# Making the context's keys and values for two layers in one process of lower rank, kept in DRAM

## The chip, the cores and the metric

The kernel runs on one core of a Trainium2 chip. The time is device microseconds of one launch. Engines are named as in the profile: PE (TensorE matmuls), PEld (its weight loads), DVE (VectorE), ACT (ScalarE), POOL (GpSimd), SP (SyncE, which issues the DMAs here; SPq is its queue).

## The reference

Two decoder layers over 128 sequences of 64 tokens, each token 128 numbers wide, float32. Six residual blocks follow one another; each is fed the layer-normalised `x`:

```
x = x + mamba2_and_mlp(norm(x))
x = x + pointer_attention(norm(x), ctx, ids, pointers)   # reads ctx
x = x + ternary_ffn(norm(x))
x = x + causal_attention(norm(x))                        # attention, convolution, attention
x = x + cross_attention(norm(x), ctx, mask)              # reads ctx
x = x + mixture_of_experts(norm(x))                      # 8 experts, top 2
```

The context `ctx_1024` has the shape of `x` and does not depend on it. Pointer attention lets each token look at three neighbouring context rows in two ways ("j" and "i"); its keys and values are `ctx @ Wkj.T`, `ctx @ Wvj.T` and the same with `i`. Cross attention has 16 heads of 8: `k = ctx @ wk`, `v = ctx @ wv`, softmax of the scores with a mask, then `@ wo`.

## The kernel before

The sequences are cut into 16 groups (`NG`) of 8 sequences (`B`), which are 512 tokens (`GT`), four tiles of 128 (`C`). A group passes ten stages in order (`LAYERS`, L199): `prepare`, `project`, `recur`, `mlp` (the mamba block), `pointers`, `ternary`, `first`, `second` (the causal block), `cross`, `experts`. `way(g)` (L1603) is the process of one group: it takes one of seven `x` buffers, loads the group, goes through the stages, and stores the result. One group at a time can be in a stage, and it leaves a stage only when the next one is free.

The order of all instructions is made while the program is built, by `Turns` (L85), a planner. Each process is a Python generator that yields

- a name: it waits for a token, such as a buffer or a stage; `turns.give(name)` gives it back, to the one who has waited longest;
- a pair of an engine and a cost in us: the instructions that follow are placed on that engine at the planned time;
- `None` and a time: it lets that much planned time pass;
- a list: child processes, all of which must end.

Among those who ask for an engine, the planner takes first the process that holds something scarce (a bank "a" or the score banks "s"), and then the one that asked first (L156, L168). The planner's order is each engine's program order on the chip. SP's instructions stand in the order in which the generators reach them.

Tokens that matter here (L196 and L200): `a`, four PSUM banks; `s`, one set of four more banks for scores; `u`, two buffers for normalised rows; `fT`, six for transposed rows; `km`, four (used by `project` to `recur`, by `first` to `second`, and by `cross`); `qm`, three; `ctxT`, two; `pT`, three sets.

What is done with the context before the change:

- In `pointers`, `group(g)` (L781) takes `ctxT` and a `u`, loads the group's context into it (L786), and runs three things side by side: `context()`, `ones()` (one-hot rows of the pointers) and `norming_T` (normalise `x`, transpose it). `context()` transposes the four tiles into `ctxT` (`turning`, L311 to L320, evacuated by ACT), stores `ctxT` to the DRAM tensor `contexts` (L802), and makes `kT` in two blocks (`keys`, L806: one 512-column matmul with `wqk` and an ACT copy each) and `vo` in two blocks (`outputs`, L815: eight small matmuls with `wvo` and an ACT copy each). `kT` and `vo` have one buffer each and no token. `kT` is read by the scores (L851) and `vo` by the last matmuls of the stage (L936); L943 then adds the result to `x`.
- In `cross`, `group(g)` (L1417) loads `ctxT` back (L1427) and runs side by side `queries()` (normalise, transpose, multiply with `wq`) and `of_context()`: `spreading` (one matmul with `wkk`, two ACT activations into `km`, L1073 to L1092) and `values` (four matmuls with `wv` and four small copies, two on DVE and two on ACT, into the tile `v_x`, whose other elements are zero; L1094). Then `attend` (L1248) reads `km` and `v_x`.
- `weights()` (L1616) prepares the weights of the later layers at the start, layer by layer, and gives each stage's token when its weights are ready.

All float32 matmuls go through the helper at L210, transposes through L317. Each float32 matmul has two records in the profile.

Of the kernel before, what the change touches and what calls it, by code (L numbers as in the profile page):

```python
# [24 lines left out]
F32 = mybir.dt.float32  # L25
# [59 lines left out]
class Turns:  # L85
# [14 lines left out]
    def give(self, name):  # L100

        self.running["scarce"] = max(0, self.running["scarce"] - (name in self.scarce))
        if self.wanted[name]:
            _, process = self.wanted[name].pop(0)
            process["time"] = max(process["time"], self.now)
            process["scarce"] += name in self.scarce
            process["engine"] = None
            self.ready.append(process)
        else:
            self.free[name].append(self.now)  # L110

    def process(self, work, time, parent):
        return dict(work=work, time=time, parent=parent, scarce=0, engine=None, n=0)

    def step(self, process):
        self.running = process
        while True:
# [21 lines left out]
            elif isinstance(item, list):  # L139
                process["children"] = len(item)  # L140
                for work in item:
                    self.ready.append(self.process(work, process["time"], process))
                return
            else:
                engine, length = item
                if engine is None:
                    process["time"] += length
                    process["engine"] = None
                    continue

                process["at"] = process["time"]
                if engine is process["engine"]:
                    process["at"] -= self.LAG
                else:
                    process["engine"], process["n"] = engine, self.n
                self.asked.setdefault(engine, []).append((process["scarce"] < 1, process["n"], process, length))  # L156
                return

    def run(self, works):
        self.ready = [self.process(work, 0.0, None) for work in works]  # L160
        while True:
# [3 lines left out]
            for engine, asked in self.asked.items():  # L165
                if asked:
                    at = max(self.until.get(engine, 0.0), min(r[2]["at"] for r in asked))
                    first = min((r for r in asked if r[2]["at"] <= at), key=lambda r: r[:2])  # L168
                    if best is None or at < best[0]:
# [4 lines left out]
            self.asked[engine].remove(request)  # L174
            process, length = request[2:]
            self.until[engine] = at + length
# [6 lines left out]
def tile_decoder(ctx: ExitStack, tc: tile.TileContext, w: dict, const: bass.AP, out: bass.AP):  # L183
# [16 lines left out]
    TOKENS = dict(BUFS, a=4, s=1, pT=3, mx=3)  # L200
    TOKENS.update({name: int(i < 4) for i, name in enumerate(LAYERS)})
    counter = [0]
    pools = {}
# [38 lines left out]
    xs = [None] * NG  # L242
    contexts = dram.tile([NG * P, GT], F32, tag="contexts", name="contexts")

# [479 lines left out]
    def pointers(mp):  # L724
# [56 lines left out]
        def group(g):  # L781

            yield "ctxT"
            yield "u"
            cg = wk([P, C, P], "u", bufs=BUFS["u"])
            nc.sync.dma_start(cg, tokens(cf, g))  # L786
            ctxT = wk([P, GT], "ctxT", bufs=BUFS["ctxT"])
            idg = wk([P, C, S], "idg", I32)
            for b in range(2):
                nc.sync.dma_start(  # L790
                    idg[b * S : (b + 1) * S], ids[b, g * C : (g + 1) * C, :].partition_broadcast(S)
                )
            kT = wk([P, B, 2, S], "kT")
            vo = wk([P, B, P], "vo")
            hot = wk([P, 3, C, S], "hot")
            rid = sm([P, C], "rid")

            def context():
                yield None, 2.5
                yield from turning(ctxT, [cg[:, c, :] for c in range(C)])  # L800
                turns.give("u")
                nc.sync.dma_start(contexts[g * P : (g + 1) * P, :], ctxT)  # L802
                yield [keys(0), keys(1), outputs(0), outputs(1)]
                turns.give("ctxT")

            def keys(i):  # L806
                yield "a"
                pk = bank("a")
                yield T, 0.88
                mm(pk, wqk[:, i, :], ctxT)  # L810
                yield A, ac(512)
                A.copy(kT[:, :, i, :], pk.rearrange("p (b s) -> p b s", s=S))
                turns.give("a")

            def outputs(half):  # L815
                yield "a"
                pvo = bank("a")
                yield T, 0.95
                for j in range(4):
                    b = half * 4 + j  # L820
                    for i in range(2):
                        mm(
                            pvo[i * S : (i + 1) * S, j * P : (j + 1) * P],
                            ctxT[:, b * S : (b + 1) * S],
                            wvo[:, i, :],
                        )
                yield A, ac(512)
                A.copy(vo[:, half * 4 : half * 4 + 4, :], pvo.rearrange("p (b d) -> p b d", b=4))
                turns.give("a")

# [14 lines left out]
            uT = []  # L845
            yield [context(), ones(), norming_T(xs[g], uT)]
            yield "a"
            psc = bank("a")
            yield T, 0.95
            for b in range(B):  # L850
# [4 lines left out]
                )  # L855
            turns.give("fT")

            s3 = sm([P, 3, 2, C], "s3")
# [76 lines left out]
            for b in range(B):  # L935
# [4 lines left out]
                )  # L940
            turns.give("fT")
            yield V, dv(512)
            V.tensor_tensor(xs[g], xs[g], po_.rearrange("p (c d) -> p c d", c=C), ALU.add)  # L943
            turns.give("a")

        stages["pointers"] = group
        return ready

# [458 lines left out]
    def cross(mp):  # L1407
# [6 lines left out]
        def ready():  # L1414
            vs.extend((yield from value_tiles(mp, "x", 1)))

        def group(g):  # L1417

            mask = wk([P, B, S], "mask")
            for i in range(2):  # L1420
# [3 lines left out]
                )  # L1424
            yield "ctxT"
            ctxT = wk([P, GT], "ctxT", bufs=BUFS["ctxT"])
            nc.sync.dma_start(ctxT, contexts[g * P : (g + 1) * P, :])  # L1427
            v = vs[0]
            yield "km"
            km = wk([P, B, 2, S], "km", bufs=BUFS["km"])  # L1430
            yield "qm"
            qm = wk([P, B, 2, S], "qm", bufs=BUFS["qm"])
# [6 lines left out]

            def of_context():  # L1440
                yield None, 2.5
                yield [spreading(km, wkk, ctxT, k["mk"], None), values(v, ctxT, wv)]

            yield [queries(), of_context()]
            turns.give("ctxT")
            yield "fT"
            oT = wk([P, GT], "fT", bufs=BUFS["fT"])
            yield from attend(masked_weights, qm, km, v, mask, oT)
            turns.give("km")
            yield from projecting(g, oT, wo)  # L1450

        stages["cross"] = group
        return ready

# [148 lines left out]
    def way(g):  # L1603
# [10 lines left out]
        turns.give("x")  # L1614

    def weights():  # L1616

# [4 lines left out]
        for ready, names in zip(layers, (LAYERS[4:5], LAYERS[5:6], LAYERS[6:8], LAYERS[8:9], LAYERS[9:10])):  # L1622
            yield from ready()
            for name in names:
                turns.give(name)
        for _ in range(2):
            turns.give("pT")
# [4 lines left out]
    with tc.manual_schedule(engines={e.engine for e in (V, A, G, T)}):  # L1632
        turns.run([way(g) for g in range(NG)] + [weights()])

# [20 lines left out]
```

## Time and profile before

| | us |
|---|---|
| median of 3 runs (2209.86 to 2229.43) | 2220.43 |
| the profiled execution | 2218.08 |
| its span, first to last instruction | 2216.3 |
| PE busy | 1925.3 (87%) |
| DVE busy | 1489.0 (67%) |
| PEld busy | 1363.1 (62%) |
| ACT busy | 1158.7 (52%) |
| POOL busy | 1020.8 (46%) |
| mean granted TensorE clock | 0.931 |
| data moved by DMA | 53.61 MB, mean 24 GB/s |

The profile page is read from the top: busy time of each engine, then 40 equal slices of the span (each digit is a slice's busy share in tenths; PEclk is the clock that was granted to PE), then the DMA queues, then the chain of work that ended last, followed back from the last instruction, then groups of instructions by source line and tiles (busy time, mean ns of one, idle time before them and who ended it), then DMA issues with the time from issue to landing. Durations are of that one execution.

### The profile page before, as it was taken

The numbers are of one execution on the slowest core, as the hardware profiler recorded it, in microseconds if no ns is written. First come the engines' busy times: TensorE is split into PE (matmuls) and PEld (weight loads), VectorE is DVE, ScalarE is ACT, GpSimd is POOL, SyncE is SP. The second block draws the span as 40 slices with busy tenths as digits, with TensorE's granted clock in tenths as the row PEclk, the third lists the DMA queues.
The fourth block names the chain that finished last, engine by engine and source line by source line (L and its number), as shares of the span: only waits on it lengthen the run. The fifth ranks groups of instructions, "written<-read, shape, count | busy, mean of one in ns | idle before, by whom it ended". The sixth has DMA issues, their size and how long they took to land.

```text
span 2216.3 us, 56830 instructions
## 1 busy us (share of the span) xinstructions
PE 1925.3 (87%) x23920; PEld 1363.1 (62%) x23920; DVE 1489.0 (67%) x3991; ACT 1158.7 (52%) x2133; POOL 1020.8 (46%) x1258
## 2 busy tenths in 40 slices
PE   3777788889889989999998898989889999997996
PEld 1455556566656666666666576666556666675664
DVE  4577877675685676786776847777676765745353
ACT  2345456556464566556565464555655555553452
POOL 2566754743444444364545552464544533423121
PEclk9688898999999999999999899999899999998998
DMA  5011010000010010010001000000000000000000
GB/s 164 20 51 36 28 38 2 23 7 18 22 36 12 6 47 21 16 37 15 26 23 38 6 28 21 16 19 26 28 25 24 2 25 11 17 7 6 12 6 5
DMA packets 73451, 53.61 MB, mean 24 GB/s; under 512 B 30087, under 2 KB 59757, under 8 KB 73197
## 3 DMA queue, kind: packets, MB, share of 16 engines
q1 hardware_dynamic: 73196, 49.99, 7.6%
q8 instruction: 188, 3.08, 0.6%
q14 instruction: 67, 0.54, 0.1%
HBM read 41.45 MB, written 8.52 MB: 23 GB/s over the span
## 4 chain that ended last, share of the span: by engine, by line
PE 55%; DVE 26%; POOL 6%; ACT 6%; issue 3%; DMA 3%; SPq 1%; DVEq 0%; POOLq 0%; ACTq 0%
PE psa L210 38%; PE pss L210 12%; PE psa L317 4%; DVE tops L1212 4%; POOL u L325 2%; DVE amx L1167 2%; DVE pT L1155 2%; DVE x L1581 2%; DVE st L307 1%; ACT pT L1245 1%; DVE mv L308 1%; DVE sel L863 1%; DMA x<-in_x 1%; DVE s L870 1%; DVE mx L1030 1%
## 5 line engine op out<-in xcount | busy, mean ns | idle before, releaser
L325 POOL TENSOR_SCALAR u<-x,mv,rstd 128x128 f32<-128x128 f32 x320 | 252.8, 802 | 52.3 <-PE psa L317 26.0
L210 PE MATMUL psa<-fT,moe_w 128*128 128x512 f32 x512 | 257.8, 627 | 11.3 <-ACT km L559 3.1
L210 PEld LDWEIGHTS psa<-moe_w,hid 128*128 128x128 f32 x2048 | 242.5, 193 | 28.6 <-issue 19.1
L210 PE MATMUL psa<-moe_w,hid 128*128 128x128 f32 x2048 | 252.0, 279 | 2.4 <-DVE sel L863 1.7
L1559 ACT ACTIVATE hid<-psa,vcol 128x512 f32<-128x512 f32 x256 | 173.5, 689 | 147.2 <-PE psa L210 144.4
L1581 DVE SCALAR_TENSOR_TENSOR x<-psa,cw,x 128x128 f32<-128x128 f32 x512 | 143.3, 342 | 127.6 <-PE psa L210 127.5
L1169 POOL TENSOR_TENSOR pT<-pT,amx 128x512 f32<-128x512 f32 x128 | 134.6, 1055 | 185.9 <-DVE amx L1167 177.9
L286 POOL TENSOR_SCALAR rsq<-mv 128x4 f32<-128x4 f32 x96 | 24.7, 257 | 368.6 <-DVE mv L308 346.1
L1245 ACT ACTIVATE pT<-pss 128x512 f32<-128x512 f32 x256 | 132.1, 603 | 118.8 <-PE pss L210 118.7
L1212 DVE TENSOR_REDUCE tops<-pss 128x32 f32<-128x2048 f32 x64 | 146.1, 2283 | 41.3 <-PE pss L210 41.3
L1044 POOL TENSOR_SCALAR r<-h 128x512 bf16<-128x512 f32 x64 | 98.0, 1540 | 128.2 <-DVE h L1042 127.0
L210 PEld LDWEIGHTS psa<-fT,moe_w 128*128 128x128 f32 x512 | 91.3, 198 | 100.2 <-issue 59.4
L1289 DVE TENSOR_TENSOR fT<-psa,inv 128x256 f32<-128x256 f32 x96 | 40.2, 420 | 155.2 <-ACT inv L1287 154.2
L210 PEld LDWEIGHTS pss<-km,qm 32*128 32x128 f32 x3072 | 101.4, 198 | 46.7 <-issue 31.5
L210 PE MATMUL psa<-pT,cst 128*32 128x256 f32 x1536 | 119.6, 401 | 10.4 <-ACT pT L1245 2.9
L625 POOL TENSOR_TENSOR qm<-qm,km 128x256 f32<-128x256 f32 x64 | 51.6, 809 | 165.6 <-DVE qm L620 165.5
L317 PE MATMUL psa<-cst,u 128*128 128x128 f32 x448 | 83.9, 304 | 50.1 <-POOL u L325 33.9
L210 PE MATMUL pss<-km,qm 32*128 32x128 f32 x3072 | 120.6, 297 | 5.6 <-DVE pT L1155 3.5
L307 DVE BATCH_NORM_STATS2 st<-x 128x6 f32<-128x128 f32 x384 | 102.7, 267 | 20.6 <-DMA x<-in_x 20.1
L319 ACT COPY fT<-psa 128x512 f32<-128x512 f32 x112 | 65.7, 588 | 85.2 <-PE psa L317 84.8
L317 PEld LDWEIGHTS psa<-cst,u 128*128 128x128 f32 x448 | 56.0, 151 | 78.2 <-POOL u L325 43.3
L1285 ACT ACTIVATE inv<-psa 128x256 f32<-128x256 f32 x96 | 37.0, 385 | 125.9 <-PE psa L210 125.5
(282 smaller groups left out, 4621.3 us busy)
## 6 DMA issues: line engine op xcount, KB each, us to landing
pT<-steps SPq DMA_DIRECT2D x64, 256.0 KB, 4.0
x<-in_x SPq DMA_DIRECT2D x16, 256.0 KB, 2.8
mask<-in_mask_Bx1xSxS_ff SPq DMA_DIRECT2D x32, 128.0 KB, 3.0
u<-in_ctx SPq DMA_DIRECT2D x16, 256.0 KB, 2.7
contexts<-ctxT SPq DMA_DIRECT2D x16, 256.0 KB, 2.0
ctxT<-contexts SPq DMA_DIRECT2D x16, 256.0 KB
out<-x SPq DMA_DIRECT2D x16, 256.0 KB, 2.3
idg<-in_itok_BxS SPq DMA_DIRECT2D x32, 64.0 KB, 2.8
```

Source lines behind the costliest of these rows:

```text
L210: T.matmul(o, lhsT=lhsT, rhs=rhs, start=start, stop=stop)
L307: V.bn_stats(st[:, c, :], X[:, c, :])
L317: T.transpose(pt[:, c * P : (c + 1) * P], part, by)
L319: A.copy(o, pt)
L325: G.tensor_scalar(u[:, c, :], X[:, c, :], mean(c), scale[:, c : c + 1], ALU.subtract, ALU.mult)
L625: G.tensor_tensor(xc[:, :, cols], xc[:, :, cols], zs[:, :, cols], ALU.mult)
L1044: G.tensor_scalar(r2, h[:, c, :], -MAGIC, None, ALU.add)
L1169: G.tensor_tensor(s3, s3, mx.unsqueeze(2).to_broadcast([P, 8, S]), ALU.subtract)
L1212: V.tensor_reduce(mx[:, :, 0:8], banks.rearrange("p r (n s) -> p r n s", s=S), AX.X, ALU.max)
L1245: A.activation(pTs[r].rearrange("p b g q -> p (b g q)"), banks[:, r, :], AF.Exp)
L1559: A.activation(hid[:, b, :], ph, AF.Relu, bias=vec["moe_b1"][:, 2 * e + b : 2 * e + b + 1])
L1581: V.scalar_tensor_tensor(X[:, c, :], po_[:, c * P : (c + 1) * P], cw[:, c, e : e + 1], X[:, c, :], ALU.mult, ALU.add,)
```

## The change

A new process `ahead` runs beside the 16 ways and `weights`. It goes over all groups in order: it loads a group's context, transposes it into `ctxT`, and makes `kT`, `vo`, `km` and the tile `v_x` of that group, each of which it stores in a DRAM tensor of its own (`kept`). `pointers` loads `kT` and `vo` from there and `cross` loads `v_x` and `km`. `contexts` and the context's use of `u` are gone. `kT`, `vo` and `v_x` now have a token each, with one copy; `pointed{g}` and `crossed{g}` say that a group's tensors are stored; "laid" says that the pointer layer's weights are ready. Every process has a rank: `ahead` has 1, the others 0. A lower number goes first among those who wait for a token, and, after the holders of something scarce, among those who ask for an engine.

```diff
@@ Turns
         if self.wanted[name]:
-            _, process = self.wanted[name].pop(0)
+            first = min(self.wanted[name], key=lambda w: (w[1]["rank"], w[0]))
+            self.wanted[name].remove(first)
+            process = first[1]
...
-                self.asked.setdefault(engine, []).append((process["scarce"] < 1, process["n"], process, length))
+                self.asked.setdefault(engine, []).append(
+                    ((process["scarce"] < 1, process["rank"], process["n"]), process, length)
+                )
@@ tile_decoder
+    TOKENS.update(ctxT=1, kT=1, vo=1, v_x=1, laid=0)
+    TOKENS.update({f"{name}{g}": 0 for name in ("pointed", "crossed") for g in range(NG)})
...
-    contexts = dram.tile([NG * P, GT], F32, tag="contexts", name="contexts")
+    kept = {
+        (name, g): dram.tile([P, n], F32, tag=f"{name}{g}", name=f"{name}{g}")
+        for name, n in (("kT", B * 2 * S), ("vo", B * P), ("km", B * 2 * S), ("v_x", B * 4 * 48))
+        for g in range(NG)
+    }
@@ pointers
         def group(g):
-            yield "ctxT"
-            yield "u"
-            cg = wk([P, C, P], "u", bufs=BUFS["u"])
-            nc.sync.dma_start(cg, tokens(cf, g))
-            ctxT = wk([P, GT], "ctxT", bufs=BUFS["ctxT"])
+            yield f"pointed{g}"
+            yield "kT"
+            kT = wk([P, B, 2, S], "kT", bufs=1)
+            nc.sync.dma_start(kT.rearrange("p b i s -> p (b i s)"), kept["kT", g])
+            yield "vo"
+            vo = wk([P, B, P], "vo", bufs=1)
+            nc.sync.dma_start(vo.rearrange("p b d -> p (b d)"), kept["vo", g])
...
-            yield [context(), ones(), norming_T(xs[g], uT)]
+            yield [ones(), norming_T(xs[g], uT)]
...
             turns.give("fT")
+            turns.give("kT")
...
             turns.give("fT")
+            turns.give("vo")
...
+        def of_context(g, ctxT):
+            def stored(name, ap):
+                nc.sync.dma_start(kept[name, g], ap)
+                yield None, 3.0
+                turns.give(name)
+            def keys():
+                yield "kT"
+                kT = wk([P, B, 2, S], "kT", bufs=1)
...
+                yield [of_one(i) for i in range(2)]
+                yield from stored("kT", kT.rearrange("p b i s -> p (b i s)"))
+            def outputs():
+                yield "vo"
+                vo = wk([P, B, P], "vo", bufs=1)
...
+                yield [of_four(half) for half in range(2)]
+                yield from stored("vo", vo.rearrange("p b d -> p (b d)"))
+            yield [keys(), outputs()]
+            turns.give(f"pointed{g}")
@@ cross
         def ready():
-            vs.extend((yield from value_tiles(mp, "x", 1)))
+            yield None, 0.1
+
+        def of_context(g, ctxT):
+            if not vs:
+                vs.extend((yield from value_tiles(mp, "x", 1)))
+            def keys():
+                yield "km"
+                km = wk([P, B, 2, S], "km", bufs=BUFS["km"])
+                yield from spreading(km, wkk, ctxT, k["mk"], None)
+                nc.sync.dma_start(kept["km", g], km.rearrange("p b i s -> p (b i s)"))
+                yield None, 3.0
+                turns.give("km")
+            def of_values():
+                yield "v_x"
+                yield from values(vs[0], ctxT, wv)
+                nc.sync.dma_start(kept["v_x", g], vs[0])
+                yield None, 4.0
+                turns.give("v_x")
+            yield [keys(), of_values()]
+            turns.give(f"crossed{g}")
...
-            yield "ctxT"
-            ctxT = wk([P, GT], "ctxT", bufs=BUFS["ctxT"])
-            nc.sync.dma_start(ctxT, contexts[g * P : (g + 1) * P, :])
+            yield f"crossed{g}"
+            yield "v_x"
             v = vs[0]
+            nc.sync.dma_start(v, kept["v_x", g])
             yield "km"
             km = wk([P, B, 2, S], "km", bufs=BUFS["km"])
+            nc.sync.dma_start(km.rearrange("p b i s -> p (b i s)"), kept["km", g])
...
-            yield [queries(), of_context()]
-            turns.give("ctxT")
+            yield from queries()
...
             turns.give("km")
+            turns.give("v_x")
@@ the processes
+    def ahead():
+        def loaded(g):
+            cg = wk([P, C, P], "ctxT", bufs=2)
+            nc.sync.dma_start(cg, tokens(cf, g))
+            return cg
+        yield "laid"
+        following = loaded(0)
+        yield None, 2.5
+        for g in range(NG):
+            cg = following
+            ctxT = wk([P, GT], "ctxT", bufs=2)
+            yield from turning(ctxT, [cg[:, c, :] for c in range(C)])
+            if g + 1 < NG:
+                following = loaded(g + 1)
+            yield [stages["pointers ahead"](g, ctxT), stages["cross ahead"](g, ctxT)]
...
+            if "pointers" in names:
+                turns.give("laid")
...
-        turns.run([way(g) for g in range(NG)] + [weights()])
+        turns.run([(0, way(g)) for g in range(NG)] + [(0, weights()), (1, ahead())])
```

## The prediction

> **What bounds the kernel.** I read the engine sums first, then the forty slices, then the chain that ended last, then a table of stretches.
>
> ```profile
> PE 1925.3 (87%) x23920; PEld 1363.1 (62%) x23920; DVE 1489.0 (67%) x3991; ACT 1158.7 (52%) x2133; POOL 1020.8 (46%) x1258
> PE   3777788889889989999998898989889999997996
> PEclk9688898999999999999999899999899999998998
> DMA  5011010000010010010001000000000000000000
> PE 55%; DVE 26%; POOL 6%; ACT 6%; issue 3%; DMA 3%; SPq 1%; DVEq 0%; POOLq 0%; ACTq 0%
> ```
>
> The first row gives TensorE (PE) 87% of the span. The slices (55.4 us each) show that this is not even: 3, then 7s, then 8s and 9s. DMA is nearly empty after the first slice. The chain runs through PE for 55% of the time and through VectorE (DVE) for 26%. The same by stretches (columns: stretch, length, then busy us of PE, PEld, DVE, ACT, POOL with counts, granted clock, DMA share, GB/s):
>
> ```profile
> 27.00:60.00 33.00, 14.94 (x42) 7.53 (x42) 21.42 (x57) 10.75 (x18) 12.51 (x14) 0.84 0.49 149
> 60.00:120.00 60.00, 44.56 (x198) 29.02 (x199) 35.66 (x109) 21.17 (x41) 33.99 (x48) 0.69 0.11 36
> 120.00:300.00 180.00, 139.09 (x1132) 95.27 (x1129) 141.91 (x381) 94.25 (x170) 117.28 (x150) 0.84 0.10 31
> 300.00:820.00 520.00, 461.42 (x6258) 328.55 (x6262) 369.67 (x948) 291.71 (x537) 257.44 (x310) 0.94 0.07 20
> 820.00:2100.00 1280.00, 1166.09 (x15372) 831.33 (x15368) 867.71 (x2321) 696.02 (x1290) 570.33 (x695) 0.95 0.07 20
> ```
>
> I cut at 27 us because L777, the last step of the pointer layer's weights, runs at 27.0 to 27.2: there "laid" is given and the new process may start. I cut at 820 because the eighth group enters `pointers` there, after a pause since 710. From 820 to 2100 PE is 91% busy, so the late part is limited by PE work. From 27 to 820 PE stands idle 18.1 + 15.4 + 40.9 + 58.6 = 133 us. If the 9% idle of the late part is what the schedule can't use anywhere, the excess is 15.1 + 10.0 + 24.7 + 11.8 = **62 us**: room for work that waits for no group.
>
> **What is moved.** No compute instruction is added or removed. The context's instructions leave `pointers` and `cross` and go into `ahead`. Their rows:
>
> ```profile
> L210 PE MATMUL psa<-wvo,ctxT 128*64 128x128 f32 x512 | 34.7, 288 | 2.3 <-DVE fT L1289 1.2 <-ACT kT L812 1.1
> L210 PE MATMUL psa<-ctxT,wqk 128*128 128x512 f32 x64 | 34.0, 646 | 2.4 <-ACT ctxT L319 2.0 <-ACT r2T L319 0.3
> L210 PE MATMUL psa<-ctxT,x_wk 128*128 128x512 f32 x32 | 17.5, 627 | 0.0
> L210 PE MATMUL psa<-x_wv,ctxT 128*128 128x128 f32 x128 | 17.0, 275 | 0.0
> L1086 ACT ACTIVATE km<-psa,cst 128x512 f32<-128x512 f32 x32 | 20.3, 689 | 8.6 <-PE psa L210 8.5
> ```
>
> The number behind the bar is busy time with overlaps counted once; mean ns times count would count the pipelined matmuls several times. With the 64 context transposes of the 448 in L317's row (83.9 x 64/448 = 12.0), PE has 34.7 + 34.0 + 17.5 + 17.0 + 12.0 = 115 us, 7.2 per group. The same question for the matmuls on `ctxT` alone, by stretches, shows when:
>
> ```profile
> 120.00:300.00 180.00, 14.03 (x108) 8.04 (x108) 1.75 (x3) 0.84 0.10 31
> 300.00:820.00 520.00, 27.06 (x194) 18.39 (x194) 2.33 (x4) 0.94 0.07 20
> 820.00:2100.00 1280.00, 56.59 (x424) 34.87 (x424) 5.47 (x9) 0.95 0.07 20
> ```
>
> After 820 lie 56.6 + 1.9 (the tail) = 58.5 us of matmuls and 9 x 0.75 = 6.7 of transposes: **65 us**. ScalarE (ACT) carries about 4.9 us per group (0.6 transposed context, 1.1 `kT`, 1.2 `vo`, 1.3 `km`, 0.7 `v_x`), DVE 0.8. Both have more slack than PE in every stretch.
>
> **When it can run.** Free of rivals an `ahead` round costs 7.2 us of PE, some evacuation behind it and a store of about 3: I estimate 12 us, so about seven groups between 27 and 120, were the engines free; at the lower rank I take five. Then `pointers` holds `kT` until its scores and `vo` until its last matmul, so about one round per pointer group: seven more by 710. In the pause from 710 to 820 the rest follows. Nearly all 65 us so come before 820.
>
> **What a late microsecond is worth.** By the row (91% busy) removing 65 us of PE saves 65 x 0.91 = 59. The Trainium skill (Perfetto Trace Analysis, Identifying the Most-Contended Engine) speaks against that: matmul busy time is a poor measure of how full TensorE is; take the LDWEIGHTS share instead. That is 831/1280 = 65% here, so PE would have a third to spare and the saving would be 65 x 0.65 = 42. The chain's 55% would give 36. The slices leave no hole as long as the rule suggests, and PE executes in order, so I stay nearer the row: **52**, ends 36 and 59.
>
> **What the early part pays.** 65 us go into 62 us of usable gaps. A low-rank step is not interrupted, and once it holds a bank ("scarce") it goes ahead of normal work that holds none. I take two thirds as hidden and 22 us as delay; ends 0 (all fits) and 65 (none fits). If the gaps weren't there, this would cancel the gain.
>
> **DMA.** Rows of before:
>
> ```profile
> contexts<-ctxT SPq DMA_DIRECT2D x16, 256.0 KB, 2.0
> u<-in_ctx SPq DMA_DIRECT2D x16, 256.0 KB, 2.7
> cst<-in_constants SPq DMA_DIRECT2D x1, 522.5 KB, 3.5
> SPq L802 <- ACT ctxT L319: 60.4, 9, 21.0
> SPq L1427 <- DMA contexts<-ctxT: 4.6, 2, 2.9
> ```
>
> Gone: 32 transfers of 256 KB (8.4 MB). Added per group: four stores and four loads of 512, 512, 512 and 768 KB, so 128 transfers, 75 MB; the total goes from 53.6 to about 120 MB and the DMA share from 8% to some 18%. From 256 KB in 2.7 us and 522 KB in 3.5 I estimate a 512 KB load at 3.5 and `v_x` at 4.3. `kT` and `vo` (1 MB, about 5 us together) load while the group is normalised, whose four centring steps alone take 3.2 us on POOL after the moments; `v_x` and `km` (1.25 MB, 6 us) likewise before `attend`. Hidden; uncovered, at most 3 us per stage, 16 x 2 x 3 = 96, but only if normalising took no time. Issuing costs SP 128 x 0.4 = 51 us spread over the span, on a queue that mostly stands waiting. 64 stores now wait in SP's queue for an evacuation, as L802 does already (9 waits), and the transfers behind them (x, `pT<-steps`, mask) wait too. The order follows the planner's time, so I take 5 us; ends 0 and 50 (3 us for each of 16 groups).
>
> **New waits.** A pointer group now starts only with `pointed{g}`, `kT` and `vo` in hand; everything of its stage is behind them, and `ternary` behind that. When a group has made its last read of `vo`, `ahead` takes it for two matmul blocks (2.2), two evacuations (1.2) and the store (3.0): 6.4 us with free banks. By the trace, from the last read of `vo` to the next group's context copy there are 6, 5, 22, 6, 21, 23 and 116 us. So three of the first entries are late by a few us, if banks are free: I take 8; ends 0 and 100. `v_x` is similar (4 us store, behind it `cross`), with the projection and the wait for `experts` as cover: 4. `km` (4 copies) is lent for some 8 us a round: nothing, below 10.
>
> **What becomes free.** Before, the context sat in one of only two `u` buffers, from its load until it was transposed (2.7 + about 3 us), while the same group's normalisation wanted the other. In every group `kT` and `vo` were complete 8 to 45 us before the first score matmul, so the context chain itself was never last; the normalised rows were. They can now start earlier. 16 x 6 = 96 us of `u` come free; I take a sixth of it for the path, as six groups share it: 15, ends 0 and 40.
>
> **Sum**, against the profiled execution (2218.1; span 2216.3, 1.8 around it): -52 + 22 + 5 + 8 + 4 - 15 = -28. So 2190. The median of the runs, 2220.4, is 0.1% above the profiled one, so 2190 stands against it too: -1.4%. About 1% (22 us) is what a measurement here can tell from none.
>
> **Rivals.**
> *A. The low rank starves and blocks the higher one* (slower, **2255**, 0.23). A process of low rank that holds `vo` while it waits for one of four banks blocks a pointer group, and nothing raises its rank. For it: five to six groups contend for the banks, and the gaps of 5 and 6 us are small. Against it: a holder of a bank gets precedence. It decides once a hold of `vo` is above 20 us, the gap of most entries: then every entry is some 15 us late, 16 x 15 = 240, of which the stage's slack takes most (it works 70 to 105 us of each 110 to 125); a quarter is left, +60. Rounds then also keep pace with the groups instead of running ahead, so the late saving shrinks to that of the first five groups' lead, about -23: 2218 + 60 - 23 = 2255.
> *B. No change* (**2212**, 0.26). PE's pieces move, but the late part is paced by in-order waits on DVE (26% of the chain) and by the seven `x` buffers: saving 36, the early part pays 30 back: -6.
> *C. SP's queue comes late* (slower, **2250**, 0.07): 2 us on each of 16 `pT<-steps` quartets and x loads; the waits of SP above speak for it, the idle DMA against.
> The forecast has 0.44.
>
> **Range.** Low: all fits and saves 59, `u` gives 20: 2140. High: A with 10 us more of its delay left: 2265. Faster 0.44, within 1% 0.26, slower 0.30 (A and C).
>
> **What would show it.** Right: PE slices 1 to 5 rise from 7 to 8 or 9 with `wvo`, `wqk` and `x_wk` matmuls from about 30 us; no such matmul after about 900; PE's busy time unchanged within a few us; the eighth group in `pointers` at 820 to 850, and a shorter stretch from there to the end. Wrong: context matmuls until the end (A); gaps of PE in front of pointer groups' first instructions; `pT` scans or ACT copies waiting for DMA (C); PE below 88% after 820 with no shorter span (B).

## The result, and the profile after

| | before | after |
|---|---|---|
| median of the comparison (10 runs each), us | 2217.81 | 2235.36 |
| ratio, with its 95% interval | | 1.0083 (1.0065 to 1.0102) |
| the profiled execution, us | 2218.08 | 2231.89 |
| its span, us | 2216.3 | 2230.1 |
| mean granted clock | 0.931 | 0.929 |

The changed kernel is 0.8% slower: within the 1% that counted as no change, and on the other side of the forecast of 2190 (-1.4%). The two profiled executions differ by 13.8 us.

The page of the changed kernel, in the order of the prediction: sums of each engine, slices of PE, granted clock and DMA, the chain that ended last.

```profile
PE 1927.3 (86%) x23920; PEld 1362.2 (61%) x23920; DVE 1483.8 (67%) x3991; ACT 1162.2 (52%) x2133; POOL 1027.8 (46%) x1258
PE   3687679889999899988889897899988999998896
PEclk9787889999999998999999897999988999999988
DMA  6333122121121113020111210010110100001000
PE 52%; DVE 27%; ACT 7%; POOL 6%; DMA 4%; issue 3%; SPq 1%; DVEq 0%; POOLq 0%; ACTq 0%
```

PE's busy time is the same within 2 us, as it had to be. The slices did not do what was announced: slices 1 to 5 were 7 7 7 7 8 and are 6 8 7 6 7, not 8s and 9s. Only DMA changed plainly (120.75 MB, 16% of the DMA engines' time): its row has digits almost throughout. PE's share of the chain fell from 55% to 52%, and DVE's and ACT's rose by one point each.

The context's own instructions on PE, by the stretches of the prediction (columns: stretch, length, busy us of PE, PEld and ACT with counts, clock, DMA share, GB/s). The transposes are included here, since the loaded context is now a `ctxT` too.

```profile
27.00:60.00 33.00, 9.08 (x50) 4.94 (x50) 0.59 (x1) 1.00 0.69 209
60.00:120.00 60.00, 18.23 (x104) 11.01 (x104) 1.76 (x3) 0.72 0.33 122
120.00:300.00 180.00, 32.76 (x210) 20.80 (x210) 2.34 (x4) 0.83 0.32 111
300.00:820.00 520.00, 34.59 (x244) 19.86 (x244) 2.95 (x5) 0.97 0.17 56
820.00:2100.00 1280.00, 27.76 (x192) 16.22 (x192) 1.76 (x3) 0.94 0.13 41
```

They start in the first stretch, but 27.8 us are still done after 820, where before had 65. So some **37 us** of PE moved across that mark, not 65. A round's second `vo` evacuation ended at 53, 93, 115, 128, 160, 215, 278, 369, 441, 452, 582, 734, 851, 954, 1065 and 1220 us. The prediction had five rounds by 120, where three were done and the fourth at 128, and the last before 900, where three were still to come.

Two rows of the table by stretches of the changed kernel (busy us of PE, PEld, DVE, ACT, POOL), to be held against 27 to 60 and 120 to 300 of before:

```profile
27.00:60.00 33.00, 16.93 (x83) 9.83 (x83) 11.81 (x38) 10.14 (x20) 0.00 (x0) 1.00 0.69 209
120.00:300.00 180.00, 132.00 (x774) 88.44 (x773) 121.71 (x350) 90.00 (x172) 105.90 (x136) 0.83 0.32 111
```

In the first, PE gained 2 us, though 9 us of context were put there, DVE fell from 21.4 to 11.8 and POOL from 12.5 to nothing. In the second, 33 us of context went in where some 16 were (14.0 of matmuls and three transposed contexts of 0.75), and PE's sum *fell* from 139.1 to 132.0. The context did not fill gaps. It took the place of the groups' work, which came later.

**The sum by one mark.** Before's eighth group enters `pointers` at 820 us, after's at 858. Cut there, before (first fence) and after (second) read (columns as in the table by stretches: stretch, length, busy us of PE, PEld, DVE, ACT, POOL with counts, clock, DMA share, GB/s):

```profile
60.00:820.00 760.00, 645.08 (x7585) 452.83 (x7589) 547.24 (x1435) 407.12 (x747) 408.72 (x507) 0.90 0.08 24
820.00:2216.30 1396.30, 1261.04 (x16288) 899.55 (x16280) 913.58 (x2475) 738.78 (x1365) 593.05 (x721) 0.95 0.06 19
```

```profile
60.00:858.00 798.00, 681.55 (x8139) 476.87 (x8140) 567.45 (x1506) 446.34 (x831) 433.58 (x538) 0.92 0.22 76
858.00:2230.10 1372.10, 1224.57 (x15687) 872.36 (x15684) 897.86 (x2421) 703.65 (x1280) 586.34 (x701) 0.93 0.11 36
```

PE's busy sum is 36.5 us lower in the later part (1261.0 to 1224.6) and 36.5 us higher in the earlier one (645.1 to 681.6). The later part became 24 us shorter (1396.3 to 1372.1), the earlier 38 us longer (760 to 798): +14, the whole difference. PE's idle time in the earlier part, which was to take in two thirds of the moved work, stayed as it was: 114.9 us before (760 - 645.1), 116.5 after.

The 36.5 us are a net figure, since the granted clock moved too, from 0.90 to 0.92 where work came in and from 0.95 to 0.93 where it left. Busy time times clock in the later part is 1261.0 x 0.950 = 1198 before and 1224.6 x 0.930 = 1139 after: some 59 us of work at full clock left it. Of these, some 42, as busy time, are the context's (65 us behind the mark before, 22.8 after); the rest is other work of groups that stand elsewhere at the mark.

The mark matters: group by group, the stores of the results (`way`, last line) are at +30, +16, +24, +4, -3, +62, +30, -10, +66, +52, +35, +31, +19, +18, +17 and +14 us against before. So 38 and 24 are one reading, not constants; that the loss arises early and is only partly earned back holds from most of these marks.

**A wait that nobody had costed.** The timeline of the changed kernel around the first context (columns: start, duration, engine, line, instruction; in brackets the idle time before it and who ended it):

```profile
33.98 4.65 SPq L290 DMA_DIRECT2D moe_b<-in_L_ffn_b  x1
38.68 0.39 SPq L1672 DMA_DIRECT2D ctxT<-in_ctx  x1
43.96 1.09 PE L328 MATMUL psa<-cst,ctxT 128*128 128x128 f32 x4 [11.90 <-DMA ctxT<-in_ctx]
45.81 0.25 DVE L477 RECIPROCAL wp<-wp 128x16 f32<-128x16 f32 x1 [11.36 <-ACT lw L474]
```

SP issues in the order in which the generators reach it. The first context load was written when "laid" was given, but it stands behind the later layers' weight loads, the last of which takes 4.65 us to issue. It goes out at 38.7. The planner had placed the transposes 2.5 us after "laid", and PE, which executes in order, waits 11.9 us in front of them. DVE stands idle behind it, through an ACT instruction (`lw`): the reciprocal at 45.8 ran at 34.3 before.

### The profile page after: what moved, and what is told of

It reads as the page before. It is cut to its first block, busy times and chain, and to the rows that moved or that the text cites. A ratio compares the mean times of both kernels' runs of the same rounds, so it can differ in the third digit from the quotient of the medians.

```text
span 2230.1 us, 57104 instructions
## 1 busy us (share of the span) xinstructions
PE 1927.3 (86%) x23920; PEld 1362.2 (61%) x23920; DVE 1483.8 (67%) x3991; ACT 1162.2 (52%) x2133; POOL 1027.8 (46%) x1258
## 2 busy tenths in 40 slices
DMA packets 87278, 120.75 MB, mean 54 GB/s; under 512 B 31622, under 2 KB 61292, under 8 KB 87020
## 4 chain that ended last, share of the span: by engine, by line
PE 52%; DVE 27%; ACT 7%; POOL 6%; DMA 4%; issue 3%; SPq 1%; DVEq 0%; POOLq 0%; ACTq 0%
PE psa L217 35%; PE pss L217 12%; PE psa L328 4%; DVE tops L1242 2%; POOL u L336 2%; DVE amx L1197 2%; DVE pT L1185 2%; DVE x L1632 2%; DVE st L318 2%; DVE mv L319 1%; DMA x<-in_x 1%; DVE sel L841 1%; ACT pT L1275 1%; DVE s L848 1%; DVE h L1051 1%
## 5 line engine op out<-in xcount | busy, mean ns | idle before, releaser
L336 POOL TENSOR_SCALAR u<-x,mv,rstd 128x128 f32<-128x128 f32 x320 | 264.2, 838 | 40.4 <-DVE r L1039 18.6
L217 PE MATMUL psa<-pT,cst 128*32 128x256 f32 x1536 | 112.1, 395 | 9.1 <-ACT pT L1275 1.7
L328 PE MATMUL psa<-cst,u 128*128 128x128 f32 x384 | 75.9, 309 | 45.0 <-POOL u L336 35.3
L1201 ACT ACTIVATE pT<-pT 128x512 f32<-128x512 f32 x128 | 77.8, 630 | 42.7 <-POOL pT L1199 41.9
L1185 DVE TENSOR_TENSOR pT<-pss,mask 128x512 f32<-128x512 f32 x128 | 87.2, 681 | 17.4 <-PE pss L217 17.2
```

The lines of the kernel that those rows point to most:

```text
L217: T.matmul(o, lhsT=lhsT, rhs=rhs, start=start, stop=stop)
L328: T.transpose(pt[:, c * P : (c + 1) * P], part, by)
L336: G.tensor_scalar(u[:, c, :], X[:, c, :], mean(c), scale[:, c : c + 1], ALU.subtract, ALU.mult)
L1185: V.tensor_tensor(sco, banks[:, r].rearrange("p (b h s) -> p b h s", b=4, s=S), mask[:, 4 * quad : 4 * quad + 4, :].unsqueeze(2).to_broadc ...
L1201: A.activation(sco, sco, AF.Exp)
```

## The experiments

### 1. The stall at the start

`e1` makes the first load before it waits for "laid", and lists `ahead` in front of `weights`:

```diff
-        yield "laid"
         following = loaded(0)
         yield None, 2.5
+        yield "laid"
...
-        turns.run([(0, way(g)) for g in range(NG)] + [(0, weights()), (1, ahead())])
+        turns.run([(0, way(g)) for g in range(NG)] + [(1, ahead()), (0, weights())])
```

> The first context load is put into SP's queue ahead of the weight loads, nothing else is changed. Theory 'start stall': in the changed kernel PE stands 11.9 us for that load and the first group is 17 us late after it; without the stall the whole run is about 12 us shorter, near 2223. Theory 'borrowed vo': the main loss is pointer groups 5 and 6 that wait 57 and 83 us for vo; then this edit brings at most a few us, 2230 to 2236.

Measured: 2227.33 us, 1.0014 (1.0000 to 1.0028) of before. Its timeline:

```profile
17.55 0.69 SPq L1672 DMA_DIRECT2D ctxT<-in_ctx  x1
32.62 1.09 PE L328 MATMUL psa<-cst,ctxT 128*128 128x128 f32 x4
```

The load is out at 17.6, and the transposes run at 32.6 with no idle time in front of them. Group 0 is stored 14 us earlier than in the changed kernel (+16 against before, where that had +30), and the end is 0.7% earlier. In the traces of the changed kernel and of `e1`, PE, VectorE, ACT and POOL execute the same instructions in the same order (23920 records of PE, 3991 instructions of VectorE, for example), so what differs is SP's order alone: the stall is real and can be removed. Two later pairs that differ by the same edit, again with one compute order each (`e2` with `e13`, `e3` with `e7`), show 0.4% and 0.1%, so at the end it is worth 3 to 15 us. Cut at its own entry of the eighth group (848), `e1` reads:

```profile
60.00:848.00 788.00, 680.16 (x8139) 477.75 (x8139) 561.59 (x1495) 442.99 (x825) 423.39 (x528) 0.92 0.23 76
848.00:2222.50 1374.50, 1226.35 (x15682) 875.40 (x15680) 896.81 (x2415) 703.75 (x1279) 585.75 (x701) 0.93 0.11 36
```

Without the stall the earlier part is still 28 us longer than before's for 35 us more of PE, and the later part 22 us shorter. PE's idle time in the earlier part is 107.8 us, 7 less than before.

### 2. The context's work left out, and the same work added

`e2` makes the context's tensors for group 0 only and lets every group load these: 15 of 16 groups' context work (and its stores) is left out, the loads and waits stay. Since every group then uses the context of group 0, these two kernels are of use for their time alone. `e13` is `e2` with the early first load of `e1`.

```diff
-        for g in range(NG):
+        for g in range(1):
...
-            nc.sync.dma_start(kT.rearrange("p b i s -> p (b i s)"), kept["kT", g])
+            nc.sync.dma_start(kT.rearrange("p b i s -> p (b i s)"), kept["kT", 0])
```

> The process ahead makes only the first group's tensors, and every group loads those; the context work of 15 groups (about 108 us of PE, 74 us of ACT) is left out, the loads stay. Theory 'the late part is limited by PE work': below 2130. Rival 'paced by waits elsewhere': above 2180, since less PE work then hardly helps. It also gives the bound of what hiding this work can bring.

> The kernel with one round for all groups (the context work of 15 groups left out), and its first load ahead of the weights. Theory 'start stall': 12 to 15 us shorter than with the stall (ratio 0.993), so about 0.987. It bounds what hiding all of the context work can bring: about 30 us of 108 us of PE.

Measured: 0.9928 (0.9905 to 0.9952) and 0.9888 (0.9857 to 0.9918). Removing 115 x 15/16 = 108 us of PE outright, from early and late, saves 25 us in `e13`: **0.23 us per us**. If the DMA that stays costs all the 11 us of experiment 5, it is 36/108 = 0.33. The prediction had 0.8. The sums of `e13`:

```profile
PE 1865.2 (85%) x23170; PEld 1315.4 (60%) x23170; DVE 1473.6 (67%) x3961; ACT 1092.0 (50%) x1998; POOL 1030.7 (47%) x1258
```

PE's busy sum fell by 60 us, not by 108, while its granted clock fell from 0.931 to 0.912, so that the instructions that are left took longer (in before's trace, `psa<-wout,qm` matmuls one behind the other start 112 ns apart where the clock is 1.0 and 213 ns where it is 0.5). Busy time times clock is 1925.3 x 0.931 = 1792 before and 1865.2 x 0.912 = 1701 here, 91 less at full clock, or 98 at before's.

`e5` goes the other way: before, with 16 rounds of the same matmuls and evacuations on a constant, in a process of rank 1, with no token but a bank and with no DMA.

```diff
+            yield from turning(fill, [ident] * C)
+            yield [one(0), one(1), four(), four()]
...
+        turns.run([(0, way(g)) for g in range(NG)] + [(0, weights()), (1, ahead())])
```

> The kernel before, with 16 added rounds of low rank that do the instructions of ahead on a constant and write into a spare tile: no kept tensors, no DMA, no kT, vo, km or v_x token. The contexts are still made in their stages. Added: about 110 us of PE and 80 us of ACT. Theory 'PE work is worth little, the waits set the pace': 10 to 35 us slower than before. Rival 'PE work sets the pace, gaps hold 62 us': 50 us or more slower. If it costs under 5 us, then filling is free and all of the loss lies in tokens, start stall and DMA.

Measured: 1.0251 (1.0235 to 1.0267), with all rounds between 33 and 758 us.

```profile
PE 2016.9 (89%) x24720; PEld 1421.7 (63%) x24720; DVE 1502.2 (66%) x4023; ACT 1233.9 (54%) x2277; POOL 1024.3 (45%) x1258
```

96 us more of work at full clock (2016.9 x 0.936 = 1888, against 1792) cost 56 us of time, so about 0.5 us per us of the 115 added. The first four groups are stored 25, 15, 18 and 8 us later. Low rank didn't hide this work, though it waited for no token but a bank and for no transfer. The clock rose to 0.936.

The two experiments took opposite sides of their expectations: by leaving work out, waits elsewhere set the pace; by adding it, PE work does. Both kernels also have an order of instructions of their own, and experiment 6 shows such an order alone moving before by up to 0.8%, or 18 us. With that to either side, `e13` (the 11 us included) gives at most 54/108 = 0.5 and `e5` at most 74/115 = 0.64, both below the prediction's 0.8; a swing as large as the late start's there (over 3%) would leave even that open. The values themselves are not settled.

### 3. Who holds `vo`

Rival A said that a low-rank holder of `vo` would block the pointer groups. It does. The rows of `vo` around the worst entry in the changed kernel (columns: durations min/median/max in ns, first and last start in us):

```profile
L217 PE MATMUL psa<-vo,fT x32: 272/273/323, 515.0 to 652.5; 128*64 128x128 f32 x32
L966 ACT COPY vo<-psa x4: 567/586/599, 560.8 to 733.6; 128x512 f32<-128x512 f32 x4
L799 SPq DMA_DIRECT2D vo<-vo x2: 319/322/326, 584.3 to 736.8; - x2
```

A pointer group (group 6, counted from 0) read `vo` for the last time at 652.5; the next one could load its own at 736.8, since `ahead` held the buffer until its evacuation at 733.6. The entry wait, counted from when a group's own `mlp`, the group ahead in `pointers` and the one ahead of that in `ternary` are all done to its first one-hot instruction, was 16, 5, 5, 4, 11, 56, 83, 20, 9, 6, 7, 9, 22, 2, 3 and 4 us for the 16 groups; before it was 10, 2, 4, 3, 8, 4, 14, 8, 19, 8, 12, 0, 11, 1, 3 and 2.

`e3` raises the rank while one of the four buffers is held, and `e7` adds the early load. `e8` is `e7` with `vo` taken by the pointer group only after its scores. `e4` gives `ahead` rank 0 throughout.

```diff
                 yield "vo"
+                turns.running["rank"] = 0
                 vo = wk([P, B, P], "vo", bufs=1)
```

> Once a child of ahead holds kT, vo, km or v_x it has rank 0 until it gives it back; the work is the same. Theory 'borrowed vo': the holds of some 60 to 80 us in front of pointer groups 5 and 6 shrink to about 10, and the run is 20 to 40 us shorter, 2195 to 2215. Theory 'start stall' or 'DMA traffic': no change, 2230 to 2240.

> The two mends of the changed kernel together: first context load ahead of the weight loads, and rank 0 while kT, vo, km or v_x is held. If the two effects are separate, their gains add (0.7% and 0.35%): ratio to before 0.998, 4 us faster than before. If the rank only moved the same waits elsewhere: as with the first load alone, 1.001 or more.

> As the two mends, and a pointer group takes and loads vo only after its scores, so its start no longer waits for vo. Theory 'the wait at the entry of pointers still costs': 5 to 15 us faster than the two mends alone. Rival 'those waits are absorbed by other groups': the same within 5 us.

> ahead has rank 0 like the groups. Theory 'low rank starves': no long holds, and all rounds done before 900; late part shorter, but the first groups are slowed more: 2200 to 2230. Rival 'contention in the first part is the loss': slower than the changed kernel, 2245 or more.

Measured: `e3` 1.0048 (1.0027 to 1.0069), `e7` 1.0036 (1.0024 to 1.0049), `e8` 1.0080 (1.0064 to 1.0096), `e4` 1.0141 (1.0118 to 1.0164). In `e3` and `e7` no entry up to group 13 waits more than 21 us, so the holds in front of groups 5 and 6 are gone. Groups 14 and 15 wait 78 and 55 us (79 and 53 in `e7`), but `ahead` is done by then (its last `vo` is evacuated at 866 and 855 us); by the same count before at `LAG` 0.15, which has no token for `vo`, has waits of 62, 41 and 59 us. So a long wait by this count is not always one for `vo`.

The 20 to 40 us that `e3` was to gain did not come (2235.35 us, in the range of "no change"), and the gains of the two edits did not add: `e7` was to be at 0.998. In `e8` no entry wait is above 18 us, all rounds are done by 391 us, and it is 0.4% slower than `e7`, where one theory said faster and the other the same: the time is that of the changed kernel. So the holds exist, but no kernel without them was clearly faster.

`e4` finishes all rounds by 731 us, which is what the prediction wanted of the low rank, and is slower still. The end of the rounds doesn't order these kernels (391 us in `e8`, 731 in `e4`, 855 in `e7`), and apart from that of `e4` their differences from before are no larger than what experiment 6 shows for an order alone.

### 4. Starting later

`e12` is `e1` with `ahead` held back until group 0 has done its `mlp`, which is at 117 us.

```diff
+            if (g, name) == (0, "mlp"):
+                turns.give("started")
...
         yield "laid"
-        yield None, 2.5
+        yield "started"
```

> The changed kernel with the first load ahead of the weights, and ahead begins its rounds only when group 0 has left mlp. Theory 'the early rounds delay the first groups and that delay is carried to the end': group 0 is then as early as before, and the run is 5 to 15 us shorter than with the load first alone (2227). Rival 'early rounds are the cheapest': pointer groups wait for their tensors, 10 us or more longer.

Measured: 2204.34 us, 0.9920 (0.9890 to 0.9950), below both kernels; group 0 is stored 18 us earlier than before instead of 30 later. It is tested further in experiment 6, where it doesn't hold.

### 5. The transfers

`e6` adds eight DRAM copies per group to before, of the sizes of the change, with nothing that they depend on.

```diff
+            for n in range(4):
+                traffic(f"tp{n}", g, 8)
```

> The kernel before, with four added transfers of 512 KB at each group's start of pointers and two of 512 KB and two of 768 KB at its start of cross, from the context into unused DRAM tensors: the number and size of transfers that the change adds, with nothing waiting for them. Theory 'DMA traffic and SP's queue cost': 10 us or more slower than before. Rival 'the DMA is free': within 4 us of before.

Measured: 1.0092 (1.0073 to 1.0112). Its DMA slices, and VectorE's wait for the scan's input (us in all, times, longest):

```profile
DMA  7487992000010010010000000000000000000000
DVE pT L535 <- DMA pT<-steps: 13.2, 2, 11.0
```

The copies were all issued in the first 343 us, not along the span as in the change, so this does not measure the change's traffic. But the compute order is that of before, and it shows something else: after the wait of 11.0 us, which ends at 341 us, group 0 is stored 14 us late and every later group 12 to 22 (the last 16).

`e11` ties them to the data: before stores `kT`, `vo`, `km` and `v_x` of each group when they are made, and copies the previous group's from DRAM to DRAM, 64 and 60 transfers beside its own.

```diff
+        nc.sync.dma_start(kept[name, g], ap)
+        if g:
+            nc.sync.dma_start(kept[name, g - NG], kept[name, g - 1])
```

> The kernel before, with kT, vo, km and v_x of each group also stored in DRAM after they are made (64 stores), and a DRAM copy of the group before's of the same sizes (64 copies): the change's traffic at the place where the stages are, nothing waits for it but the next writer of a tile. Planner and order of the compute engines as before. Theory 'the traffic costs': 8 us or more slower. Rival 'free': within 4 us of before.

Measured: 1.0048 (1.0032 to 1.0064), so +11 us.

```profile
DVE pT L541 <- DMA pT<-steps: 9.1, 4, 6.3
```

Before waited 1.9 us there. The order of the compute instructions is again that of before. The delay comes at one place: the wait of 6.3 us ends at 1219 us, and from the seventh group on the results are late (the stores are at 2, 2, -3, 0, 1, 2, 11, 11, then 9 to 13 us to the end).

### 6. How much any other order moves

The planner's `LAG` (0.2 us) is what it allows between the end of one step and the next of its process. Changing it changes no instruction, only the order.

```diff
-    LAG = 0.2
+    LAG = 0.25
```

> The kernel before with one constant of its planner changed (LAG, the planned time between two engines, 0.2 to 0.25 us): the same instructions in a slightly different order. It measures how much a new plan alone moves the time. If plans are alike: within 3 us of before. If the order alone moves the time as much as the mends did: 8 us or more, either way.

> The kernel before with the planner's LAG at 0.15 us instead of 0.2: a third plan of the same instructions. If the plan of before is a lucky one: 5 us or more slower, as with 0.25 (+0.8%). If 0.25 was an unlucky one: within 5 us of before, or faster.

> The changed kernel with LAG 0.25. Theory 'the change itself costs (start stall, early rounds)': slower than before with LAG 0.25, 1.013 or more. Rival 'its +0.8% is within the lottery and the change is neutral': between 1.000 and 1.010.

> The late start with LAG 0.25. Theory 'the late start gains beyond the lottery of plans': faster than before with the same LAG (ratio 1.0083), at or below 1.000. Rival 'its 0.992 was luck': 1.008 or more.

> The late start with LAG 0.15. Theory 'gains beyond the lottery': about 0.5 to 1% under the kernel before with LAG 0.15. Rival 'luck': at or above it.

| ratio to before as it is | LAG 0.15 | 0.2 | 0.25 |
|---|---|---|---|
| before | 0.9969 (0.9954 to 0.9984) | 1 | 1.0083 (1.0050 to 1.0115) |
| after | not run | 1.0083 (1.0065 to 1.0102) | 1.0103 (1.0081 to 1.0125) |
| late start (`e12`) | 1.0245 (1.0223 to 1.0268) | 0.9920 (0.9890 to 0.9950) | 1.0111 (1.0069 to 1.0152) |

An arbitrary constant moves before by up to 0.8% (1.1% from end to end), as much as the change did, and the late start by over 3%. At 0.25 before and after differ by 0.2%. The gain of `e12` is one order's, not the idea's. The same doubt lies on every kernel here with an order of its own (`e3` with `e7`, `e4`, `e5`, `e2` with `e13`, `e8`) against before; it doesn't lie on pairs with one compute order (after and `e1`, `e2` and `e13`, `e3` and `e7`, before with `e6` and `e11`).

In `e16` one pointer group waited 138 us for `vo` (last read at 927.6, the next pair of evacuations ends the hold after 1077.8), and the results that had been up to 75 us early came up to 70 us late:

```profile
L217 PE MATMUL psa<-vo,fT x16: 272/273/323, 926.8 to 927.6; 128*64 128x128 f32 x16
L966 ACT COPY vo<-psa x4: 586/586/587, 825.5 to 1077.8; 128x512 f32<-128x512 f32 x4
```

So I tried the raised rank on the late start, at LAG 0.15 and 0.2:

> The late start at LAG 0.15, and a child of ahead has rank 0 while it holds kT, vo, km or v_x. Without that, pointer group 8 waited 138 us for its vo and the first groups' lead of 65 us was gone: 1.0245. Theory 'borrowed vo sets a bad plan's time': the wait is under 40 us and the run 40 us or more shorter, 1.006 or less. Rival 'the lottery of plans has nothing to do with the holds': 1.015 to 1.03.

> The late start at LAG 0.2 with rank 0 while holding. Its holds of 56 and 83 us at pointer groups 5 and 6 should shrink to 20. Theory 'borrowed vo': faster than the late start alone (0.992), 0.98 to 0.99. Rival 'a new plan is a new ticket': anything between 0.99 and 1.015.

Measured: `e18` 1.0388 (1.0361 to 1.0415), `e19` 1.0012 (0.9993 to 1.0030). In `e18` the longest entry wait is 45 us, and it is the slowest kernel of all: the theory that the borrowed `vo` sets the time fails here too. The sums and the clock of `e16`:

```profile
PE 1951.4 (86%) x23920; PEld 1379.1 (61%) x23920; DVE 1479.1 (65%) x3991; ACT 1162.5 (51%) x2133; POOL 1024.6 (45%) x1258
PEclk9688897998999999999997899898898998899988
```

Busy time times clock is 1951.4 x 0.915 = 1786, against 1792 before: the work is the same, and PE's larger sum goes with its lower clock.

## Why the prediction was wrong

**The early part (22 us for 65) failed first.** It took 62 us of PE's idle time before 820 as room and hid two thirds of the context in it. By the mark, `e1` paid 28 us for 35 moved, a fifth hidden, where one third was to be paid (12 us), and only 7 us of PE's 115 us of idle time there were filled, in after none. PE's sum in 120 to 300 *fell* with some 17 us of context more. The step's other end (all paid, "this would cancel the gain") was near the truth. In before's trace that idle time is no free stretch but many short waits for what VectorE, POOL and ACT make; the three largest from 60 to 820 us are (us in all, times, longest):

```profile
PE psa L317 <- POOL u L325: 12.4, 13, 5.9
PE psa L1217 <- DVE tops L1212: 11.6, 6, 4.4
PE psa L210 <- DVE xdt L603: 10.7, 9, 2.2
```

Why the context's blocks did not fit into them was not isolated. Each needs one of the same four banks and an evacuation, and a step that isn't interrupted can delay the group whose input arrives meanwhile; `e5` shows that the first groups are delayed without any token but a bank and without a transfer, not which of these does it.

**The worth of a late microsecond (0.8) was too high.** By the mark it is 24/36.5 = 0.66 in after and 22/35 = 0.63 in `e1`; by `e13`, over the whole span, 0.23 to 0.33. Per us of work at full clock the first is 24/59 = 0.41, nearer to the second and to the 0.5 of `e5`. The row's 91% and the chain's 36 of 65 were both above these, as was the weight-load share of 0.65 that the prediction took after the Trainium skill (Perfetto Trace Analysis, Identifying the Most-Contended Engine); that it lies near 0.66 is chance, as 0.66 is of busy time at two clocks, and the page offers the share as a measure of TensorE's headroom, not of what a us is worth. One thing that no share contains is that part of what is taken off PE comes back in its clock (0.95 to 0.93 after the mark, 0.912 in `e13`). The skill's page TensorE: Matmul & The Clock Gate, Part 1 on the HAM clock gate, says that the throttled clock is the default and activity releases it; the rows go that way (0.936 with work added, 0.912 with work removed), but no run here changed the gaps alone.

**The amount (65 us) was 37.** The rounds kept pace with the pointer groups through the single `vo` and the low rank, as rival A had it; with the rank raised during a hold (`e3`) they were done by 866. `e4` moved all of it and was slower, so moving more did not bring the gain.

**The first load was missing from the sum.** "Of a step that is moved" I costed the transfers, but not where the first stands in SP's queue: 11.9 us of PE, 14 at group 0, 3 to 15 at the end. This is the one term that runs with one compute order show by themselves, and by this pair's ratios it is most of what the changed kernel lost (1.0083 with it, 1.0014 without).

**Smaller terms.** DMA, taken at 5, is 11 by `e11`, of the mechanism of rival C (waits for `pT<-steps` 1.9 to 8.4 us, for x 20.1 to 28.0), here in the list of waits of the changed kernel (us in all, times, longest):

```profile
DVE st L318 <- DMA x<-in_x: 28.0, 10, 5.5
PE psa L328 <- DMA ctxT<-in_ctx: 11.9, 1, 11.9
DVE pT L541 <- DMA pT<-steps: 8.4, 2, 6.6
```

The landing times were about right: 4.3 and 3.5 estimated, and from the issues of the changed kernel (KB, median us to landing):

```profile
v_x<-v_x SPq DMA_DIRECT2D x32, 768.0 KB, 4.0
kT<-kT SPq DMA_DIRECT2D x32, 512.0 KB, 3.2
vo<-vo SPq DMA_DIRECT2D x32, 512.0 KB, 2.9
km<-km SPq DMA_DIRECT2D x32, 512.0 KB, 3.9
```

The entry waits for `vo`, taken at 8 us in three places, were 52 and 69 us above before's for two groups, and `e8` without them was not faster. The credit of 15 for the freed `u` buffers was not isolated; no run put the context elsewhere and left the rest. Its reading that `kT` and `vo` were complete 8 to 45 us before the first score matmul is 5.5 to 42 us in the trace, which changes nothing.

**The sum again**, with what was measured: late part -24, early part without the stall +28 (its DMA in it), stall +10 (38 - 28) = +14, the profiled difference. That it closes follows from cutting at one mark; the runs that stand by themselves are the stall (`e1`), the worth (`e13`, `e5`) and the DMA (`e11`).

By its time the result lies between B (2212) and A (2255); by its reasoning it is nearest to B: pieces move, and what is saved late is paid early. A's blocked entries happened without a price of A's size that a run could show.

**Open:** beside the stall, how much of the missing 28 us belongs to the change and how much to the order it happened to get, as a change of `LAG` moves before by 0.8%; the term for `u`; and why some orders (`e16`, `e18`) are 2 to 4% slower at the same work.

## What to carry to other kernels

Before moving work off a busy engine, leave the work out once and add it once: these two ratios give a scale for what moving can bring, and here even removing 15 of 16 rounds was worth only 1.1%. For a process that starts early, find its first load's place in the issuing queue, because an engine that executes in order waits for it with everything behind, as PE did here for 11.9 us. Where an offline planner sets the order, run it with a few arbitrary constants first, and take no difference below that spread for an effect, unless both kernels execute their instructions in the same order.

## What was not expected of the hardware

- TensorE's busy time times its granted clock was nearly the same for the same work in every order (1792 before, 1793 in `e9` with 1943.0 x 0.923, 1786 in `e16`; 1782 to 1801 in all the profiles with this work), while the clock went from 0.911 (`e18`) to 0.931. The orders with most idle PE time have the lowest clock (329 us and 0.911 in `e18`, 328 and 0.915 in `e16`, against 291 and 0.931 before) and a larger busy sum. A larger sum is then no sign of more work.
- The load of a small bias (`moe_b`, 8 rows of 128 numbers) took 4.65 us to issue on SP, against 0.39 for the context load behind it. Why is not shown.
- With the compute order unchanged, one wait of 11.0 us at 341 us left all 16 groups late (12 to 22 us in `e6`, 16 at the end), and one of 6.3 us all groups from the seventh on (9 to 13 us in `e11`), though PE is idle for 290 us of the span.
